# Values times probabilities in column tiles, with row sums on VectorE, one activation table set and shorter 3x3 blocks, in a four-layer convolution kernel

## The chip, the cores and the metric

One core of one Trainium2 chip. The metric is the device time of one execution in microseconds, lower is better. The kernel was timed three times; each time is that of the only core. A profiled execution gives a trace of every instruction on the five engines: TensorE (PE, with its weight loads PEld apart), VectorE (DVE), ScalarE (ACT), GpSimd (POOL) and SyncE (SP, which here only issues DMAs).

## The reference

The input x has shape (4, 384, 64, 64), float32. Four layers follow each other, each as x = x + layer(group_norm(x)) with 32 groups. What the change touches lies in the first three:

```python
# layer 0: attention over 4096 positions on the first 96 channels
q, k, v = qkv[:, :16], qkv[:, 16:32], qkv[:, 32:]          # 16, 16, 96 channels
attn = softmax(einsum('bcn,bcm->bnm', q, k) * scale, axis=-1)
out = einsum('bcn,bmn->bcm', v, attn)
xm = relu(concatenate([out, x_skip], axis=1))               # x_skip: other 288 channels
y = _bn(einsum('oc,bchw->bohw', w_proj, xm))

# layer 1: 1x1, filter in 8x8 Fourier patches, 3x3 depthwise, gated gelu, 1x1
t = einsum(x, w_in); t = irfft2(rfft2(patches(t)) * fft_filter)
t = depthwise3x3(t, w_dw)
g = gelu(t[:, :192]) * t[:, 192:]
return einsum(g, w_out)

# layer 2: depthwise 3x3 and 5x5 side by side, mixed by gates, then an MLP
y3 = _bn(_dw(x, c3_w, 1)); y5 = _bn(_dw(x, c5_w, 2))
tok = _bn(kw[:, 0:1] * y3 + kw[:, 1:2] * y5 + x * c1_w + c1_b)
h2 = _bn(gelu(_bn(tok * gates @ cm_w1)) @ cm_w2)
return gate * (tok * gates + h2) + (1 - gate) * x
```

Layer 3 is a 7x7 depthwise convolution whose kernel depends on the image.

## The kernel before

All arithmetic is in float32. The program is written with tiles and pools; a planner puts the instructions of each engine in an order, by priority (the order of the program, if nothing else is said) and by when it expects their inputs, sets the semaphores, and gives out buffers. On the chip each engine then runs its list in that order. `tc.high_priority()` lifts what is written inside it ahead of older work.

Four stages follow each other.

Attention with layer 1 beside it (`phase_a`, `attention`, `layer1`). For each of four images, 8 blocks of 512 query positions by 8 groups of 512 key positions make 64 steps. A step has:

- scores (L755): four matmuls of 32 contraction rows, each in its own quarter of PE's rows, 128 keys by 512 queries each, into a PSUM tile of four banks that exists once (`p4`, tag "s"). They are written inside `tc.high_priority()`;
- Exp on ACT (L763): two instructions of 128x1024 into `probs` (two buffers). No maximum is subtracted, except where a bound on the weights fails;
- products (L792): four matmuls that accumulate in the PSUM tile `av` (tag "a", two buffers). The stationary operand `vt` is 128 keys by 128 columns: 96 channels of values, and 32 columns of ones, so that rows 96 to 127 of `av` are the sums of the probabilities.

The scores of step n+1 are written ahead of the products of step n. After the eighth key group `finish` takes a reciprocal of the 32 rows of sums (L775) and multiplies it into the 96 rows of values by three instructions of 32 rows (L778); `layer0_end` follows with the projection (L825), the residual (L832) and statistics.

`side_by_side` puts other work between the steps, piece by piece, by a budget in microseconds per step: the statistics of the next image (`x_norm`), its q, k, v (`qkv`), and layer 1 of the image before. Layer 1 works on tiles of 128 positions: `tile_norm` (on DVE, L903, while attention runs; on ACT, L901, for the last image, which has no attention beside it), `tile_hidden` (L911), `tile_filter` (L926, L928), `tile_back` (L936, L939), then `band_taps` with 27 multiply-adds on DVE per band of 8 rows (L988), two gelus (L992, L995), and `band_out` (L1005, L1006, L1009). The PSUM tag "m" that all this shares has two buffers.

The last image's layer 1 alone.

The convolutions of layer 2 (`phase_b`): 12 units of 32 channels, each in 16 rounds of two channels. For a channel, three matmuls (L1196) take a 128x128 piece of the image strips as the stationary operand and banded tap matrices of 256 columns (128 for 5x5, 128 for 3x3) as the moving one. The tap matrices are made on DVE and POOL by turns (`matrices53`, L1177) from compact taps that `_pair` lays out; results leave PSUM by one ACT copy (L1205) and feed statistics (L1208), go to memory, come back in another layout (`unit_tok`, L1261 to L1282) and are mixed.

The MLP of layer 2 (`phase_ef`, L1420, L1472) and layer 3 (`phase_g`).

Every reciprocal root is Ln followed by Exp on ACT (`rsqrt`, L354, L355). The activation tables that ACT needs are loaded by instructions put in at compile time ahead of a function that the loaded set lacks.

Of the kernel before, what the change touches and what calls it, by code (L numbers as in the profile page):

```python
# [40 lines left out]
UNITS = C // 32  # L41

# [154 lines left out]
def _pair(u, v):  # L197

    return np.stack([u, v], axis=4)
# [69 lines left out]
class _Builder:  # L269
# [60 lines left out]

    def open_psum(self, ctx, m_bufs=4):

        self.psum = ctx.enter_context(self.tc.tile_pool(name="psum", bufs=2, space=bass.MemoryType.PSUM))
        self.m_bufs = m_bufs
# [49 lines left out]
    def bn_of_four(self, name, z, g, b, func, out):  # L384
# [8 lines left out]
        nc.scalar.activation(out, z, func, bias=c, scale=a)  # L393
# [31 lines left out]
    def qkv_weights(self, pool):  # L425
# [23 lines left out]
        self.wv = pool.tile([PD + 1, P], F32, tag="wv", name="wv")  # L449
# [3 lines left out]
        nc.gpsimd.memset(self.wv[PD : PD + 1, PD:], 1.0)  # L453
# [3 lines left out]
        nc.vector.tensor_copy(self.wv[:, 0:PD], wt[:, 32:P])  # L457
# [27 lines left out]
    def phase_a(self, strips):  # L485
# [3 lines left out]
        with ExitStack() as ctx:  # L489
            self.open_psum(ctx, 2)  # L490
            cp = ctx.enter_context(tc.tile_pool(name="a_const", bufs=1))
# [20 lines left out]
            self.score_shifts(cp)  # L512
            self.w_proj = self.weight(cp, "w_proj_t")
# [43 lines left out]
    def others(self, b, nxt):  # L557
# [3 lines left out]
        if b + 1 < B:  # L561
            yield from self.x_norm(b + 1)
# [7 lines left out]
    def side_by_side(self, b, steps, others):  # L570

        per_step = ((176 if b else 0) + (42 if b + 1 < B else 0)) / 64
# [74 lines left out]
    def qkv_tiles(self):  # L647
# [4 lines left out]
        vt = self.big.tile([P, 32, P], F32, tag="vt", name="vt", bufs=2)  # L652
        return q, k4, vt

    def qkv(self, b, q, k4, vt):
# [8 lines left out]
        for i in range(8):  # L664
# [18 lines left out]
            mv = m.rearrange("p (c d) -> p c d", d=P)  # L683
# [59 lines left out]
    def attention(self, b, q, k4, vt):  # L743
# [5 lines left out]
        def scores(i, c):  # L749
            p = self.probs.tile([P, 2048], F32, tag="p", name="probs")  # L750
            s = self.p4("sc_s")

            with tc.high_priority():
                for g in range(4):
                    nc.tensor.matmul(  # L755
                        s[:, g],
                        lhsT=k4[32 * g : 32 * g + 32, c],
                        rhs=q[i][32 * g : 32 * g + 32],
                        start=True,
                        stop=True,  # L760
                    )
# [9 lines left out]
        def finish(av):  # L771

            xm = self.work.tile([P, NJ, 512], F32, tag="xm", name="xm", bufs=1)
            rd = self.wk("av_rd", "rd", 1)
            nc.vector.reciprocal(rd[PD:P], av[PD:P])  # L775
            for g in range(3):
                at = slice(32 * g, 32 * g + 32)
                nc.vector.scalar_tensor_tensor(xm[at, 0], av[at], 0.0, rd[PD:P], ALU.max, ALU.mult)  # L778
# [6 lines left out]
        for n_step, (i, c) in enumerate(steps):  # L785
# [3 lines left out]
            if c == 0:  # L789
                av = self.pa("av")  # L790
            for v in range(4):
                nc.tensor.matmul(  # L792
                    av,
                    lhsT=vt[:, 4 * c + v, :],
# [1121 lines left out]
```

## Time and profile before

| | us |
|---|---|
| median of three runs | 4928.02 |
| lowest, highest | 4917.86, 4933.94 |
| profiled execution | 4921.93 |
| its span, first to last instruction | 4920.2 |

| stretch of the profile | from, to (us) | what runs |
|---|---|---|
| prologue | 0 to 128 | constants, first image's statistics and q, k, v |
| attention, four images | 128 to 2225 | steps, with qkv and layer 1 between them |
| last image's layer 1 | 2225 to 2490 | bands, and the first strips |
| convolutions | 2490 to 3095 | 12 units |
| MLP and layer 3 | 3095 to 4920 | |

A group of the profile is a set of instructions of one line, engine, operation and shape, with busy time, mean length of one, and the idle time of the engine just before them with what ended it. Matmuls are pipelined, so the length of one is more than the distance to the next; and a float32 matmul shows as two records. The mean granted TensorE clock was 0.961.

### The profile page before, as it was taken

The numbers are of one execution on the slowest core, as the hardware profiler recorded it, in microseconds if no ns is written. First come the engines' busy times: TensorE is split into PE (matmuls) and PEld (weight loads), VectorE is DVE, ScalarE is ACT, GpSimd is POOL, SyncE is SP. The second block draws the span as 40 slices with busy tenths as digits, with TensorE's granted clock in tenths as the row PEclk, the third lists the DMA queues.
The fourth block names the chain that finished last, engine by engine and source line by source line (L and its number), as shares of the span: only waits on it lengthen the run. The fifth ranks groups of instructions, "written<-read, shape, count | busy, mean of one in ns | idle before, by whom it ended". The sixth has DMA issues, their size and how long they took to land.

```text
span 4920.2 us, 47066 instructions
## 1 busy us (share of the span) xinstructions
PE 4484.3 (91%) x17289; PEld 2510.4 (51%) x17289; DVE 2787.8 (57%) x4506; ACT 2155.9 (44%) x2905; POOL 777.6 (16%) x593
## 2 busy tenths in 40 slices
PE   5999999999999999999978999699999997678988
PEld 2333444334443344435467888344444443577888
DVE  5322566645656345565867778555521113667898
ACT  5444444555445544445245666311123334753321
POOL 1000000000000000000035555000000001225554
PEclk9999999999999999999989999799999998788999
DMA  5210211111122111113259999776664444896776
GB/s 176 69 46 28 92 58 60 61 60 47 56 70 67 47 33 65 65 62 112 83 169 282 288 295 299 250 270 254 250 240 153 154 152 143 309 343 195 234 252 229
DMA packets 345844, 752.21 MB, mean 153 GB/s; under 512 B 22683, under 2 KB 172294, under 8 KB 336646
## 3 DMA queue, kind: packets, MB, share of 16 engines
q1 hardware_dynamic: 279864, 475.07, 31.4%
q0 software_dynamic: 32640, 151.28, 7.9%
q10 hardware_dynamic: 33102, 122.77, 6.4%
q8 instruction: 140, 2.29, 0.2%
q14 instruction: 98, 0.80, 0.1%
HBM read 446.76 MB, written 302.25 MB: 152 GB/s over the span
## 4 chain that ended last, share of the span: by engine, by line
PE 67%; DVE 13%; ACT 8%; DMA 7%; issue 4%; POOL 1%; SPq 0%; ACTq 0%; DVEq 0%; POOLq 0%
PE av L792 14%; PE h_s L1420 10%; PE h_m L1472 9%; PE conv_m L1196 9%; PE sc_s L755 5%; PE proj_m L825 4%; PE t_m L911 3%; DVE acc L988 3%; PE out_m L1006 2%; PE conv_m L1786 2%; PE out_m L1005 2%; PE back_m L936 2%; DMA wmix<-in_mix_t 1%; ACT probs L763 1%; DMA g_h<-h 1%
## 5 line engine op out<-in xcount | busy, mean ns | idle before, releaser
L792 PE MATMUL av<-probs,vt 128*128 128x512 f32 x2048 | 964.6, 606 | 0.1
L763 ACT ACTIVATE probs<-sc_s 128x1024 f32<-128x1024 f32 x512 | 501.1, 1021 | 721.3 <-PE av L792 717.9
L792 PEld LDWEIGHTS av<-probs,vt 128*128 128x128 f32 x2048 | 369.7, 192 | 467.9 <-issue 460.5
L1196 PE MATMUL conv_m<-toep,z 128*128 128x256 f32 x2304 | 520.1, 385 | 10.3 <-DVE toep L1177 6.4
L988 DVE SCALAR_TENSOR_TENSOR acc<-band,vecs,acc 128x512 f32<-128x512 f32 x708 | 496.6, 746 | 45.7 <-POOL band L949 40.0
L1472 PE MATMUL h_m<-f_h,cm_w_t 128*128 128x512 f32 x1152 | 496.6, 594 | 8.8 <-ACT f_h L1462 8.7
L1196 PEld LDWEIGHTS conv_m<-toep,z 128*128 128x128 f32 x2304 | 439.0, 193 | 71.7 <-DVE z L1129 4.9
L1786 PE MATMUL conv_m<-toep,z 128*128 128x128 f32 x3072 | 391.4, 285 | 40.5 <-POOL toep L1773 21.6
L1786 PEld LDWEIGHTS conv_m<-toep,z 128*128 128x128 f32 x3072 | 377.0, 201 | 42.8 <-POOL toep L1773 22.0
L1177 POOL TENSOR_TENSOR toep<-w,band 128x1536 f32<-128x1536 f32 x94 | 323.8, 3445 | 281.7 <-PE conv_m L1196 240.8
L1420 PE MATMUL h_s<-e_tok,cm_w_t 128*128 128x512 f32 x768 | 362.6, 594 | 5.5 <-DMA e_tok<-tok 5.5
L1472 PEld LDWEIGHTS h_m<-f_h,cm_w_t 128*128 128x128 f32 x1152 | 219.3, 191 | 286.1 <-issue 273.5
L755 PE MATMUL sc_s<-q,k 32*128 32x512 f32 x2048 | 296.5, 648 | 25.7 <-ACT probs L763 25.2
L1480 DVE BATCH_NORM_STATS2 h_st<-f_h 128x6 f32<-128x512 f32 x96 | 66.4, 694 | 429.2 <-ACT f_h L1479 429.2
L911 PE MATMUL t_m<-w_in_t,xb 128*128 128x384 f32 x768 | 276.4, 494 | 4.7 <-DVE coef L928 3.5
L825 PE MATMUL proj_m<-xm,w_proj_t 128*128 128x512 f32 x576 | 269.4, 606 | 9.4 <-DVE xm L778 6.5
L1427 ACT COPY e_h<-h_s 128x1024 f32<-128x1024 f32 x96 | 97.2, 1012 | 400.8 <-PE h_s L1420 400.8
L832 DVE SCALAR_TENSOR_TENSOR x_res<-proj_m,bn_c,x_res 128x512 f32<-128x512 f32 x96 | 71.7, 747 | 308.7 <-PE proj_m L825 308.7
L1420 PEld LDWEIGHTS h_s<-e_tok,cm_w_t 128*128 128x128 f32 x768 | 146.5, 191 | 189.7 <-issue 183.6
L1429 DVE BATCH_NORM_STATS2 h_st<-e_h 128x6 f32<-128x512 f32 x192 | 123.5, 685 | 199.5 <-ACT e_h L1427 199.5
L911 PEld LDWEIGHTS t_m<-w_in_t,xb 128*128 128x128 f32 x768 | 142.3, 191 | 141.0 <-issue 58.0
L1420 PE MATMUL h_s<-z,cm_w_t 128*128 128x512 f32 x384 | 196.1, 592 | 0.0
(392 smaller groups left out, 6119.3 us busy)
## 6 DMA issues: line engine op xcount, KB each, us to landing
d<-d_o ACTq DMA_DIRECT2D x96, 512.0 KB
c_d<-d SPq DMA_DIRECT2D x96, 512.0 KB
hid<-e_h ACTq DMA_DIRECT2D x16, 3072.0 KB
f_h<-hid SPq DMA_DIRECT2D x16, 3072.0 KB
x_in<-in_x SPq DMA_DIRECT2D x96, 256.0 KB
x_res<-in_x SPq DMA_DIRECT2D x32, 768.0 KB
xa<-x_res POOLq DMA_DIRECT2D x32, 768.0 KB, 3.9
xa_in<-xa SPq DMA_DIRECT2D x32, 768.0 KB
```

The lines of the kernel that those rows point to most:

```text
L755: nc.tensor.matmul(s[:, g], lhsT=k4[32 * g : 32 * g + 32, c], rhs=q[i][32 * g : 32 * g + 32], start=True, stop=True,)
L763: nc.scalar.activation(p[:, h * 1024 : (h + 1) * 1024], s[:, 2 * h : 2 * h + 2].rearrange("p a b -> p (a b)"), AF.Exp, scale=0.25,)
L792: nc.tensor.matmul(av, lhsT=vt[:, 4 * c + v, :], rhs=p[:, v * 512 : (v + 1) * 512], start=c == 0 and v == 0, stop=c == 7 and v == 3,)
L825: nc.tensor.matmul(m, lhsT=self.w_proj[:, j, o * P : (o + 1) * P], rhs=xm[:, j], start=j == 0, stop=j == NJ - 1,)
L911: nc.tensor.matmul(m[:, 0:C], lhsT=xb[:, j], rhs=self.w_in[:, j, :], start=j == 0, stop=j == NJ - 1,)
L988: nc.vector.scalar_tensor_tensor(out, src(j, k), w, done, ALU.mult, ALU.add)
L1177: eng.tensor_tensor(t, self.w53[:, at : at + 192].rearrange("p (m n) -> p m n", n=8).unsqueeze(2).to_broadcast([P, 24, 8, 8]), band.rearra ...
L1196: nc.tensor.matmul(m[:, c * 256 : (c + 1) * 256], lhsT=self.z_[:, at : at + P], rhs=t[:, 12 * c + 4 * i : 12 * c + 4 * i + 4].rearrange("p ...
L1420: nc.tensor.matmul(s[:, v, :], lhsT=w1[:, j, o * P : (o + 1) * P], rhs=t[j][:, v * 512 : (v + 1) * 512], start=j == 0, stop=j == NJ - 1,)
L1429: nc.vector.bn_stats(st[:, o, 8 * b + 2 * i + v, :], h[:, o, v * 512 : (v + 1) * 512])
L1472: nc.tensor.matmul(m, lhsT=w2[:, o, j * P : (j + 1) * P], rhs=h[:, o, v * 512 : (v + 1) * 512], start=o == 0, stop=o == 5,)
L1786: nc.tensor.matmul(m[:, ch * P : (ch + 1) * P], lhsT=self.z_[:, at : at + P], rhs=t[:, 8 * c + 2 * i : 8 * c + 2 * i + 2].rearrange("p m a ...
```

## The change

Products and sums. `vt` and `wv` lose the ones columns and are 96 wide. Each step's products are twelve matmuls of 32 columns in place of four of 128: each one of four key groups times one of three quarters of the values. A plan says which go together, one in each quarter of PE's columns, in three rounds, and into which of two PSUM tiles each accumulates.

```diff
+PLAN = (
+    ((0, 0, 3), (0, 1, 2), (0, 2, 1), (0, 0, 0)),
+    ((1, 1, 0), (0, 1, 3), (0, 2, 2), (0, 0, 1)),
+    ((1, 1, 1), (1, 2, 0), (0, 2, 3), (0, 0, 2)),
+)
...
+        def products(av, c, p):
+            quarter = lambda g: slice(32 * g, 32 * g + 32)
+            for n, jobs in enumerate(PLAN):
+                for g, (k, s, v) in enumerate(jobs):
...
+                    nc.tensor.matmul(
+                        av[k][quarter(g)],
+                        lhsT=vt[:, 4 * c + v, quarter(s)],
+                        rhs=p[:, v * 512 : (v + 1) * 512],
...
+        def add_up(c, p):
+            lo, hi = p[:, 0:1024], p[:, 1024:2048]
...
+                nc.vector.tensor_add(self.acc, self.acc, lo)
+                nc.vector.tensor_add(self.acc, self.acc, hi)
+            if c == 7:
...
+                nc.vector.tensor_add(self.prob_sum, self.acc[:, 0:512], self.acc[:, 512:1024])
```

At the end of a block the two PSUM tiles are copied out by two ACT and two DVE copies at high priority; the sums over partitions are made by four matmuls with a block of ones, laid out as 128x128, inverted by one reciprocal, and spread again over 96 partitions and 512 columns by four matmuls with a broadcast identity column. Two DVE instructions then add the halves and multiply.

```diff
+        def evacuate(av):
+            a, t = self.wk("av_a", "rd", 1), self.wk("av_t", "av_t", 1)
+            with tc.high_priority():
+                nc.scalar.copy(t[0:32], av[0][96:128])
+                nc.vector.tensor_copy(a[0:PD], av[0][0:PD])
+                nc.scalar.copy(t[32:64], av[1][0:32])
+                nc.vector.tensor_copy(t[64:96], av[1][32:64])
+            return a, t
+        def invert(total):
+            m = self.pm("sum_m")
+            for g in range(4):
+                nc.tensor.matmul(
+                    m[32 * g : 32 * g + 32, 0:P],
+                    lhsT=self.ones,
+                    rhs=total[:, g * P : (g + 1) * P],
...
+            rd = self.sm([P, P], "av_rd")
+            nc.vector.reciprocal(rd, m[:, 0:P])
-            rd = self.wk("av_rd", "rd", 1)
-            nc.vector.reciprocal(rd[PD:P], av[PD:P])
-            for g in range(3):
-                at = slice(32 * g, 32 * g + 32)
-                nc.vector.scalar_tensor_tensor(xm[at, 0], av[at], 0.0, rd[PD:P], ALU.max, ALU.mult)
+            m = self.pm("rd_m")
+            for g in range(4):
+                nc.tensor.matmul(
+                    m[0:PD, g * P : (g + 1) * P],
+                    lhsT=self.ident[:, 32 * g : 32 * g + 1].to_broadcast([P, PD]),
+                    rhs=rd,
...
+            nc.vector.tensor_add(t[0:PD], t[0:PD], a[0:PD])
+            nc.vector.scalar_tensor_tensor(xm[0:PD, 0], t[0:PD], 0.0, m[0:PD], ALU.max, ALU.mult)
...
-                av = self.pa("av")
+                av = self.pa("av_0"), self.pa("av_1")
```

The scores are no longer written at high priority. `tile_norm` runs on ACT for all images. The statistics of images 1 and 2 are made beside image 0, those of image 3 beside image 1, and the budget follows:

```diff
-        if b + 1 < B:
-            yield from self.x_norm(b + 1)
+        for later in ((1, 2), (3,), (), ())[b]:
+            yield from self.x_norm(later)
...
-        per_step = ((176 if b else 0) + (42 if b + 1 < B else 0)) / 64
+        per_step = ((172 if b else 0) + (38 if b + 1 < B else 0) + (8, 4, 0, 0)[b]) / 64
```

Tables. The set that holds both Exp and Ln is loaded on purpose at the start, and again behind the last use of any other set (gelu, sigmoid, square root). A band's two gelus stand together, behind the third tap group:

```diff
+    def ln_exp(self, behind=None):
+        load = lambda: self.nc.scalar.preload_act_table_set("natural_log_exp_and_others")
...
-            if j == 1:
-                nc.scalar.activation(acc[0], acc[0], AF.Gelu)
-                nc.vector.tensor_mul(acc[1], acc[1], acc[0])
             if j == 2:
-                nc.scalar.activation(acc[0][64:P], acc[2][0:64], AF.Gelu)
-                nc.vector.tensor_mul(acc[2][64:P], acc[2][64:P], acc[0][64:P])
+                g = self.wk("gelu", "gelu", 1)
+                with self.tc.high_priority():
+                    first = nc.scalar.activation(g[64:P], acc[2][0:64], AF.Gelu)
+                    with self.tc.issue_after(first.ins):
+                        last = nc.scalar.activation(acc[0], acc[0], AF.Gelu)
+                    self.ln_exp(last)
+                nc.vector.tensor_mul(acc[1], acc[1], acc[0])
+                nc.vector.tensor_mul(acc[2][64:P], acc[2][64:P], g[64:P])
```

Convolutions. Of the twelve tap blocks of a channel two were zero for the 3x3; `_pair` now lays out ten, a channel's middle matmul has 256 columns and the two outer ones 192, and the results leave PSUM by two copies.

```diff
-            for i in range(3):
+            for i, k0, k1, to in ((1, 3, 7, 0), (0, 0, 3, 0), (2, 7, 10, 64)):
...
-                    m[:, c * 256 : (c + 1) * 256],
+                    m[:, c * 256 + to : c * 256 + to + 64 * (k1 - k0)],
...
-        nc.scalar.copy(self.d_o[:, :, at : at + 2], mv)
+        nc.scalar.copy(self.d_o[:, 0, at : at + 2], mv[:, :, 64:192])
+        ends = mv.rearrange("p c (k n) -> p c k n", n=64)[:, :, 0:4:3]
+        nc.scalar.copy(self.d_o[:, 1, at : at + 2].rearrange("p c (f n) -> p c f n", f=2), ends)
```

## The prediction

> **What bounds the kernel now.** I read the busy shares first, then the same by stage, then the groups inside the two stages that the change touches, then the order of time for what one step costs.
>
> ```profile
> PE 4484.3 (91%) x17289; PEld 2510.4 (51%) x17289; DVE 2787.8 (57%) x4506; ACT 2155.9 (44%) x2905; POOL 777.6 (16%) x593
> DMA  5210211111122111113259999776664444896776
> ```
> ```profile
> 128.00:560.00 432.00, 413.74 (x1334) 164.79 (x1334) 139.09 (x236) 199.26 (x225) 8.82 (x14) 0.98 0.18 57
> 585.00:1110.00 525.00, 504.25 (x1649) 216.54 (x1648) 312.52 (x511) 259.87 (x317) 20.01 (x39) 0.99 0.17 58
> 1110.00:1690.00 580.00, 559.55 (x1842) 242.65 (x1841) 330.60 (x574) 288.37 (x354) 23.28 (x44) 0.99 0.17 57
> 1690.00:2225.00 535.00, 518.31 (x1690) 223.29 (x1688) 296.33 (x481) 232.02 (x283) 16.13 (x34) 0.98 0.17 56
> 2225.00:2490.00 265.00, 236.72 (x784) 121.21 (x784) 196.44 (x320) 113.47 (x215) 11.85 (x26) 0.94 0.32 106
> 2490.00:3095.00 605.00, 568.21 (x2718) 492.01 (x2718) 455.58 (x878) 360.00 (x557) 323.81 (x94) 0.97 0.91 271
> ```
> The columns are stretch, length, busy PE, weight loads, DVE, ACT, POOL, granted clock, DMA share, GB/s. The first four rows are the four batches of attention: PE 96 to 97%, DVE 32% in the first and 55 to 60% in the others, ACT near 50%. The fifth is the last image's band work alone, the sixth the 5x5 and 3x3 convolutions: PE 94%, DVE 75%, DMA 91%. So a microsecond of PE work is a microsecond of span, until DVE or DMA has no room.
>
> ```profile
> L792 PE MATMUL av<-probs,vt 128*128 128x512 f32 x2020 | 949.1, 605 | 0.0
> L763 ACT ACTIVATE probs<-sc_s 128x1024 f32<-128x1024 f32 x502 | 491.2, 1021 | 721.2 <-PE av L792 717.9 <-PE sc_s L755 2.5
> L755 PE MATMUL sc_s<-q,k 32*128 32x512 f32 x2000 | 287.4, 644 | 24.5 <-ACT probs L763 23.9
> L775 DVE RECIPROCAL av_rd<-av 32x512 f32<-32x512 f32 x32 | 107.6, 3363 | 93.0 <-PE av L792 92.7
> L778 DVE SCALAR_TENSOR_TENSOR xm<-av,av_rd 32x512 f32<-32x512 f32 x96 | 65.6, 684 | 1.9
> L763 ACT ACT_TABLE_LOAD x44 | 56.5, 1283 | 0.8
> ```
> These are groups of the attention stretch. An f32 matmul is two records. Exp waits for PE (717.9 us), PE waits for Exp 23.9 us only: PE is the bound, ACT is not.
>
> ```profile
> 1200.49 2.74 PE L825 MATMUL proj_m<-xm,w_proj_t 128*128 128x512 f32 x6
> ...
> 1203.15 1.14 PE L755 MATMUL sc_s<-q,k 32*128 32x512 f32 x8
> ...
> 1204.22 2.20 PE L911 MATMUL t_m<-w_in_t,xb 128*128 128x384 f32 x6
> ...
> 1207.77 3.60 PE L792 MATMUL av<-probs,vt 128*128 128x512 f32 x8
> ...
> 1211.20 2.74 PE L825 MATMUL proj_m<-xm,w_proj_t 128*128 128x512 f32 x6
> ```
> Start, length, count. One step's eight av records take 1211.20 - 1207.77 = 3.43 us, 0.428 each. The score group is four row tiles: eight records in one block. The proj records before it are through at 1200.49 + 6 x 0.428 = 3.06 past 1200, the next matmul starts at 4.22: the block costs 1.16 us against 2 x 0.428 = 0.86 for perfect overlap. So four tiles do run at once, and entering plus leaving the tiled form costs 0.30.
>
> ```profile
> 2730.42 20.89 PE L1196 MATMUL conv_m<-toep,z 128*128 128x256 f32 x96
> ```
> ```profile
> 4890.10 4.47 PE conv_m L1786 x40
> ```
> A 256-column record streams at 20.89/96 = 0.218 us; a 128-column one, with its own weights each time, at 0.112. Weight loads therefore keep up with records of 0.112, and a 192-column record should take 0.163.
>
> **What the Trainium skill says.** "TensorE: Matmul & The Clock Gate", Measured speedup vs the span model: four row tiles give 3.07x, three column tiles 2.38x, column within some ns of row. The trace has 3.43/1.16 = 2.96 for four row tiles; it has no column tiles that run together. "TensorEngine Tiling (Array Packing)", Key Properties: a change of tiling mode drains the array; the 0.30 above fits. "ScalarE: Activation LUTs", Table sets: exp and ln have one set in common, and a switch costs 2.66 us with its drain; the trace has 1283 ns and the next ACTIVATE right behind. "VectorE: DVE Perf Modes", Mode 2x_2P: an fp32 tensor_tensor cannot use two ports for one tensor, so 128x1024 takes twice a 128x512, which is 681 ns at L993.
>
> **The change, part by part**, against the profiled execution (4921.9; span 4920.2).
>
> *Products.* 256 steps (4 batches x 8 x 8) lose 3.43 us and gain three rounds of four column tiles. Best case 3 x 0.857 = 2.57; with the mode change of the score block 2.87; some groups stand next to scores and share the change. I take 2.83: 256 x 0.60 = -153. Bounds: 2.57 gives -220; three rounds that each drain like the score block, 3 x 1.16 = 3.48, give +13.
> *Sums.* The ones columns go, DVE adds instead: two 128x1024 adds a step, about 1.21 us each (1.14 apart, as the chain of L988 has 0.746 at 0.678 spacing), 256 x 2.42 less the shorter first step: about +600 us of DVE, 150 a batch. Gone from DVE: half-empty reciprocals 107.6 (now 128 wide, a quarter of the length, some 27), two of three L778 (-41), the band norm of L903 (82.5, to ACT); added: two PSUM copies and one add per block, 32 x 2.1 = 65. Second batch: 312 + 106 = some 420 of about 500 us, 84%; third and fourth 76 to 80%. DVE stays under PE, but its queue is in order and carries tap chains of 6 us (1208.91: nine in 6.10), so coef (L928), x_res (L832) and the release of the probs buffers come later and PE waits now and then: +25, between 0 and +90.
> *Inversion and spread on PE.* Per block eight 128-column records for rd_m at 0.112 to 0.157, and eight in column tiles for the sums, 0.22 + 0.30: about 1.5 us x 32 = +48 (35 to 60). The narrower v_m stays at its weight loads: 0.
> *Evacuation.* av now takes both "a" banks, so a block's first product waits for two ACT copies (0.58) and two DVE copies (0.68) of the block before. Behind that product stand all later PE instructions. A score block and a piece of other work, 1.1 + 3 us, cover it; if DVE is in a chain they don't: +8 (0 to 50).
> *Tables.* 144 loads in the attention stretch become some 48 (two for each of 24 bands): -123 us of ACT, given back by the band norm (288 x 0.43 = +124) and evacuation (+37). ACT stays at 50%. PE's 23.9 us of waits for Exp fall to about 14: -10. Before 128 us, 22 loads go, some on the chain of the first layer norms: -8. The twelve loads after 3095 stand in serial statistics: -6. In the stretch alone each band now loads twice, 16 x 1.28 = 20 us of ACT at 43%, and both gelus come at the end: +4 (0 to 15).
> *Scores unprioritized, budget, earlier x_norm.* Scores no longer cut an av group in two (they do at 1241.07), which saves a second mode change that column tiles would pay. No work is added; the 23.9 could rise instead: within the bounds above.
> *3x3 blocks.* A channel has 256 + 192 + 192 columns in place of 3 x 256. Two of three tap groups shrink by 0.218 - 0.163, two records each: 384 x 4 x 0.055 = -84 of PE. Beside it toep falls by a sixth, the split d_o copy costs ACT +30 (two of 0.37 for one of 0.584) against 28 loads of 1.28 that mostly go. Left after PE: DVE (455 - 28)/521 = 82%, and DMA: 164 MB in 521 us is 315 GB/s against 271 mean, 292 in the middle and 390 at best in 4 us stretches. Taken -60 (-15 to -85).
> Sum: -153 + 25 + 48 + 8 - 10 - 8 - 6 + 4 - 60 = -152. The profiled execution becomes 4770; the median of the runs shown lies 6 above it, so 4776.
>
> **Rivals.** (1) *DVE takes the bound in attention.* For it: 84% in an in-order queue, and every probs buffer (two) now waits for DVE too. Against: its sum is under PE's in each batch. Waits of 110 instead of 25: 4861. (2) *The convolutions become DMA-bound.* For it: DMA share 0.91, 0.99 in the middle. Against: DVE, ACT and POOL wait there for DMA some 33 us in all, PE hardly, and the share reads 1.2 in places, so it is no ceiling. The gain shrinks to 15: 4821. (3) *Slower: the column tiles overlap less than row tiles do.* Place: the product groups; each tile streams its own 128-partition operand, which row tiles don't. It decides from 3.42 us a step (2.83 + 152/256), that is 1.14 a round, hardly below the measured score block, so three rounds that drain each time suffice: 4776 + 256 x 0.65 = 4942. Two at a time, 5.44, give 5444; no overlap, 24 x 0.428 = 10.3, gives 6688. Against it only the skill's 2.38x.
>
> **Chances.** Forecast 0.69, rival 1 0.09, rival 2 0.07, rival 3 0.15. The forecast's bounds: all gains 4640, most costs 4900; that holds rivals 1 and 2, and leaves out rival 3 and a little. A measurement tells about 0.3% from no change. Faster 0.82 (the first three, less a sliver), within 0.3% 0.03, slower 0.15.
>
> **What would show it.** A product group should be 24 records of 32 columns in about 2.6 to 2.9 us; DVE adds near 1.2 us; DVE at 80 to 85% in batches two to four; ACT loads near 50 in attention; conv records of 192 columns at 0.163 and the stage near 545 us. Wrong: rounds of over 1.1 us; PE waits for DVE over 60 us; DMA waits in the convolutions; PE idle at each block's start before the first product.

## The result, and the profile after

The changed kernel takes 4958.01 us (median; 4943.58 to 4968.24) against 4925.86 for the kernel before on the same chips: ratio 1.0064, interval 1.0047 to 1.0080. It is slower by 0.6% where a gain of 3% was forecast. The profiled execution takes 4950.78 us (span 4948.9) against 4921.93 for the kernel before.

First the busy shares of the changed kernel (engine, busy time, share, instructions; then the DMA share over the span), then the same by stage with the columns of the stage rows shown before the result. The first four rows are the batches of attention, the fifth the last image's bands alone, the sixth the convolutions.

```profile
PE 4430.6 (90%) x21897; PEld 2370.8 (48%) x21897; DVE 3215.2 (65%) x4762; ACT 2127.7 (43%) x3310; POOL 731.0 (15%) x593
DMA  4410111111111111112349999876654444896776
```
```profile
128.00:560.00 432.00, 395.58 (x2577) 128.48 (x2574) 290.35 (x397) 191.57 (x247) 17.40 (x23) 0.95 0.22 69
560.00:1110.00 550.00, 518.09 (x2744) 195.05 (x2743) 411.99 (x563) 261.08 (x382) 20.39 (x40) 0.97 0.17 57
1110.00:1700.00 590.00, 555.82 (x2963) 208.88 (x2964) 426.77 (x589) 286.15 (x427) 22.17 (x43) 0.95 0.17 56
1700.00:2240.00 540.00, 505.32 (x2852) 190.46 (x2851) 384.73 (x499) 261.10 (x386) 15.19 (x30) 0.96 0.15 52
2240.00:2556.00 316.00, 270.47 (x854) 133.55 (x853) 225.53 (x361) 136.98 (x234) 16.51 (x30) 0.89 0.31 100
2556.00:3125.00 569.00, 502.13 (x2683) 464.20 (x2682) 426.92 (x867) 331.74 (x713) 272.39 (x94) 0.93 0.92 278
```

PE is still the bound: 92 to 94% busy in attention, DVE at 67 to 75%. But attention is not shorter, and the granted clock fell from 0.99 to 0.96 there and from 0.97 to 0.93 in the convolutions. Next, the groups of the changed kernel's attention stretch (busy time, mean ns of one, idle time before and what ended it).

```profile
L801 PE MATMUL av<-probs,vt 128*32 128x512 f32 x6076 | 745.1, 618 | 10.8 <-DVE av_t L829 7.7 <-DVE av_a L827 3.1
L786 ACT ACTIVATE probs<-sc_s 128x1024 f32<-128x1024 f32 x504 | 487.6, 1018 | 427.9 <-PE sc_s L778 402.5 <-DVE acc_p L817 15.5 <-DVE xa_st L629 7.7
L778 PE MATMUL sc_s<-q,k 32*128 32x512 f32 x2016 | 363.5, 664 | 8.9 <-ACT probs L786 8.8
L817 DVE TENSOR_TENSOR acc_p<-acc_p,probs 128x1024 f32<-128x1024 f32 x221 | 270.0, 1222 | 16.0
L816 DVE TENSOR_TENSOR acc_p<-acc_p,probs 128x1024 f32<-128x1024 f32 x221 | 269.9, 1221 | 166.1 <-ACT probs L786 165.6
```

The products fell from 949.1 us to 745.1: the column tiles do what was forecast. The scores, which issue exactly what they did before, rose from 287.4 us to 363.5. The order of time in one step of the changed kernel (start, length, engine, count, idle time before) shows how.

```profile
1218.79 0.91 PE L1003 MATMUL coef_m<-t_t,to_coef 128*128 128x384 f32 x2 [1.59 <-DVE x_res L912]
1219.63 1.13 PE L778 MATMUL sc_s<-q,k 32*128 32x512 f32 x6
1221.23 0.94 PE L1013 MATMUL back_m<-to_pos,coef 128*128 128x128 f32 x6 [0.47 <-ACT t_t L996]
1222.10 1.12 PE L778 MATMUL sc_s<-q,k 32*128 32x512 f32 x2
1223.15 2.78 PE L801 MATMUL av<-probs,vt 128*32 128x512 f32 x24
1225.86 2.84 PE L905 MATMUL proj_m<-xm,w_proj_t 128*128 128x512 f32 x6
```

One step's group of 24 product records takes 1225.86 - 1223.15 = 2.71 us. The score block of eight records is cut into six and two, with six records of a band's `back_m` between them: the piece of two takes 1223.15 - 1222.10 = 1.05 us, as long as a whole block. With the priority gone, the ordering of the instructions fills other TensorE work in between the four row tiles of a block.

The table takes each kernel's trace from the first score to the last product. A run is a stretch of records of one tile with no other between them (`av` counts as one tile); it is timed from its first record to the start of the next run, or to its own end where TensorE then idles. The last column is half of the busy time that falls into stretches with the TensorE clock at one half (the clock record knows only full and half); it lies inside the other columns. The fourth column has the number of score runs and their time. All times are us, of one profiled execution each. Some expectations quote counts that differ a little from this one, such as 777 for the products of e1 and 913 for those of e11.

| kernel | attention | products | score runs, time | PE idle | lost to half clock |
|---|---|---|---|---|---|
| before | 2136 | 923 | 256, 279 | 81 | 28 |
| after | 2177 | 737 | 318, 362 | 139 | 97 |
| after, scores in priority (e1) | 2116 | 783 | 256, 279 | 113 | 37 |
| before, scores without (e2) | 2269 | 937 | 311, 357 | 91 | 92 |
| after, sums left out (e3) | 2154 | 734 | 319, 363 | 118 | 97 |
| before, tables alone (e5) | 2111 | 919 | 256, 277 | 61 | 27 |
| before, products alone (e8) | 2182 | 805 | 256, 278 | 146 | 54 |
| e1 with a fixed order (e9) | 2087 | 770 | 256, 276 | 118 | 41 |
| before, tables, short 3x3, norm on ACT (e11) | 2108 | 917 | 256, 277 | 62 | 24 |
| e1, sums left out (e12) | 2086 | 785 | 256, 278 | 89 | 22 |

### The profile page after: what moved, and what is told of

It is laid out like the page before. It is cut to its first block, busy times and chain, and to the rows that moved or that the text cites. A ratio compares the mean times of both kernels' runs of the same rounds, so it can differ in the third digit from the quotient of the medians.

```text
span 4948.9 us, 57215 instructions
## 1 busy us (share of the span) xinstructions
PE 4430.6 (90%) x21897; PEld 2370.8 (48%) x21897; DVE 3215.2 (65%) x4762; ACT 2127.7 (43%) x3310; POOL 731.0 (15%) x593
## 5 line engine op out<-in xcount | busy, mean ns | idle before, releaser
L801 PE MATMUL av<-probs,vt 128*32 128x512 f32 x6144 | 758.3, 619 | 10.8 <-DVE av_t L829 7.7
L1276 PE MATMUL conv_m<-toep,z 128*128 128x192 f32 (+1 forms) x2304 | 447.1, 356 | 17.9 <-DVE toep L1257 17.7
L801 PEld LDWEIGHTS av<-probs,vt 128*32 128x32 f32 x6144 | 178.9, 112 | 549.2 <-issue 510.3
L1276 PEld LDWEIGHTS conv_m<-toep,z 128*128 128x128 f32 x2304 | 410.7, 197 | 40.9 <-issue 10.1
L1873 PEld LDWEIGHTS conv_m<-toep,z 128*128 128x128 f32 x3072 | 381.6, 203 | 38.2 <-POOL toep L1860 18.7
L778 PE MATMUL sc_s<-q,k 32*128 32x512 f32 x2048 | 381.6, 666 | 8.9 <-ACT probs L786 8.8
L816 DVE TENSOR_TENSOR acc_p<-acc_p,probs 128x1024 f32<-128x1024 f32 x224 | 273.6, 1221 | 167.4 <-ACT probs L786 166.8
L1257 POOL TENSOR_TENSOR toep<-w,band 128x1280 f32<-128x1280 f32 x94 | 272.4, 2902 | 310.1 <-PE conv_m L1276 196.5
L817 DVE TENSOR_TENSOR acc_p<-acc_p,probs 128x1024 f32<-128x1024 f32 x224 | 273.6, 1221 | 16.0
```

Of the source, the lines that this page charges most:

```text
L778: nc.tensor.matmul(s[:, g], lhsT=k4[32 * g : 32 * g + 32, c], rhs=q[i][32 * g : 32 * g + 32], start=True, stop=True,)
L801: nc.tensor.matmul(av[k][quarter(g)], lhsT=vt[:, 4 * c + v, quarter(s)], rhs=p[:, v * 512 : (v + 1) * 512], start=c == 0 and not before, s ...
L816: nc.vector.tensor_add(self.acc, self.acc, lo)
L817: nc.vector.tensor_add(self.acc, self.acc, hi)
L1276: nc.tensor.matmul(m[:, c * 256 + to : c * 256 + to + 64 * (k1 - k0)], lhsT=self.z_[:, at : at + P], rhs=t[:, 10 * c + k0 : 10 * c + k1].r ...
L1873: nc.tensor.matmul(m[:, ch * P : (ch + 1) * P], lhsT=self.z_[:, at : at + P], rhs=t[:, 8 * c + 2 * i : 8 * c + 2 * i + 2].rearrange("p m a ...
```

## Experiments on attention

Times are medians; each ratio is to the kernel before on the same chip.

**e1: priority back.** The changed kernel with one line more.

```diff
+            with tc.high_priority():
                 for g in range(4):
```

> The changed kernel with the priority of the score matmuls put back, nothing else. Theory A (the scores, left to the planner without priority, are cut into pieces by other TensorE work, and each piece pays entering and leaving the tiled form again): runs of score records go back from some 307 to about 250, their slot time from 345 us to about 270, and the half-clock stretches shrink with them; the kernel takes 4830 to 4890 us, 1 to 2.5% under the changed kernel. Theory B (DVE's in-order queue with 570 us of added sums makes TensorE wait, and each wait drops its clock): the waits for DVE stay near 100 us and the clock stays low; 4935 to 4965. A second rival to A: with priority the score blocks land inside the groups of products, which now pay the change of form twice as well; then the product groups grow from 2.71 us a step by what the score runs save, and the time stays within 0.3%.

4899.43 us, ratio 0.9945 (0.9929 to 0.9962). Theory A has the mechanism right: no score block is cut, their time is back at 279 us, the half clock costs 37 us, not 97, and TensorE's waits that DVE ended fall from 104 us to 86. The time lies 9 us above its range. The one line is worth 59 us: with it the change gains 28 us. The second rival has a share in it: products rise from 737 to 783, chiefly because score blocks now fall into product groups. The order of time of this kernel:

```profile
1525.16 1.90 PE L802 MATMUL av<-probs,vt 128*32 128x512 f32 x10
1526.99 1.14 PE L779 MATMUL sc_s<-q,k 32*128 32x512 f32 x8
1528.07 1.92 PE L802 MATMUL av<-probs,vt 128*32 128x512 f32 x14
1529.91 2.84 PE L906 MATMUL proj_m<-xm,w_proj_t 128*128 128x512 f32 x6
```

The two pieces take 1.83 and 1.84 us, 3.67 in place of 2.71: a cut costs 0.96 us here. What a piece costs follows the rounds that it begins, not its records (a round is four matmuls, eight records). Mean time of a run at full clock, by its records (us):

| run of | 2 | 4 | 6 | 8 | 10 | 14 | 16 | 24 |
|---|---|---|---|---|---|---|---|---|
| new products (e1) | 0.98 | - | 0.99 | 1.03 | 1.85 | 1.85 | 1.89 | 2.72 |
| old products (before) | 0.98 | 1.84 | 2.65 | 3.49 | | | | |
| scores (changed kernel) | 1.06 | 1.09 | 1.08 | 1.07 | | | | |

Two records one after another are 2 x 0.428 = 0.86. So a run of tiled matmuls costs about 0.86 for each round that it begins, plus 0.1 to 0.2 once. A cut inside a round makes one round into two, 10 + 14 records 3.70 in place of 2.72; a cut between rounds, 8 + 16, adds only 0.20; and in the old products, where nothing overlaps, 4 + 4 adds 0.19. The price of a cut is mostly lost overlap.

**e2: priority taken from the kernel before.** The reverse edit.

> The kernel before with the priority of the score matmuls taken away, nothing else: this part of the change alone. Theory A: the score blocks are split here as well, 40 to 80 more runs of about 1.05 us each, so 4965 to 5010 us, 0.8 to 1.7% slower than before. The prediction's own reading (no work is added, and product groups are cut less often): within 0.4% of before, 4910 to 4945. If splitting only comes with the changed kernel's other work (more small TensorE instructions that become ready between two halves of a score block), also within 0.4%.

5057.46 us, 1.0272 (1.0255 to 1.0289): 130 us slower, more than any theory gave. 55 more score runs cost 78 us of their own time; with them comes a half clock in 25 stretches in place of 13, and the small band groups around them lengthen. The products rise from 923 to 937, though whole groups rise from 132 to 245. So the edit costs more on the old products than on the new, which it spares 46 us. The prediction's reading ("no work is added") is excluded.

**e3: sums left out.**

```diff
-            else:
-                nc.vector.tensor_add(self.acc, self.acc, lo)
-                nc.vector.tensor_add(self.acc, self.acc, hi)
```

> The changed kernel without the sums of seven of the eight key groups: DVE adds only the first group of each block, so the probabilities are divided by the sum over 512 of 4096 keys. This takes about 224 x 2.42 = 540 us from DVE in the attention stretch and a reader of each probs buffer. Theory B: idle TensorE in attention falls from 137 to about 70 us and the half-clock loss there from 74 to some 25 us: 4840 to 4870 us. Theory A: the score runs stay at about 307 and 345 us, the time falls by no more than the waits for DVE, 20 to 50 us: 4905 to 4935.

4923.69 us, 0.9987 (0.9976 to 0.9999), that is 34 us under the changed kernel. The kernel leaves out seven of the eight key groups' sums. Idle fell by 21 us and the half-clock loss stayed at 97. Theory B is rejected as the main cause: taking 540 us from DVE gains 34.

**e8: products alone.** Products, sums, inversion, evacuation and the 96-wide `vt` in the kernel before; scores in priority, tables, band norm and budget as before.

> The kernel before with the new products, sums, inversion and evacuation alone; scores keep their priority, tables, band norm, budget and convolutions are those of before. The prediction's terms for this part: -153 + 25 + 48 + 8 = -72, so 4854, ratio 0.985. If column tiles pay for being cut by priority scores as the run above suggests (about +40 on 723 us of products) and the waits for DVE drop the clock: 4880 to 4910. If DVE, here with the band norm still on it (82 us) and 570 us of sums, takes the bound in the last three batches: above 4930.

4982.67 us, 1.0125 (1.0102 to 1.0147): 58 us slower where the prediction's terms give 72 less. By the count of the table, which has not all tiles: products -118, `rd_m` and `sum_m` +50, idle +65, and the rest in longer band groups (`t_m` 192 to 205, `back_m` 75 to 84). So TensorE's busy time falls by only 19 us (2055 to 2036), and the waits take more than that back. The longest of them, in the attention stretch of this kernel, and three in the kernel before (from 128 us to 2225; who waits, for whom: total us, times, longest):

```profile
PE sc_s L763 <- ACT probs L771: 26.3, 30, 3.4
PE back_m L1001 <- ACT t_t L984: 24.4, 14, 2.6
PE av L786 <- DVE av_t L814: 13.1, 4, 9.8
PE v_m L693 <- ACT ln_rs L361: 8.8, 8, 2.7
```
```profile
PE sc_s L755 <- ACT probs L763: 23.9, 27, 2.9
PE v_m L685 <- ACT ln_rs L354: 9.5, 6, 2.7
PE back_m L936 <- ACT t_t L919: 5.5, 5, 1.5
```

Three of the four longest are for ACT, but two of the three stood there before. Summed over attention by the engine that ended them, the waits for ACT rise from 48 us to 63 (`back_m` alone by 19), and those for DVE from 31 to 81, spread over many small ones. So most of the rise is for DVE. It is 76 to 77% busy in batches two to four, so its rate isn't the bound: the third expectation has the time right and the mechanism wrong.

**e5: tables alone.**

> The kernel before with the table part of the change alone: Ln and Exp loaded as one set, both gelus of a band moved to its last step, the set loaded again behind them; the band norm stays on DVE. As predicted (waits for Exp -10, prologue -8, statistics after the convolutions -6, last image's bands alone +4), 20 us less: 4907, ratio 0.996. If the late gelus and the load behind each of them are what lengthens the last image's bands in the changed kernel by some 20 us, this one has that too: its stretch alone 290 to 300 us against 274 and the time 4925 to 4935. If that stretch is longer for another reason (what is left over of the bands when attention ends), it stays at 270 to 278.

4892.41 us, 0.9932 (0.9908 to 0.9955): 32 us less, 25 of it in attention. The bands alone take 291 us against 274: most of what that stretch loses in the changed kernel comes with the late gelus and the load behind each band.

**e9: a fixed order.** e1, where each score block is queued behind the whole product group of the step before, and each product group behind the score block of the next step.

```diff
-            with tc.high_priority():
+            with tc.high_priority(), self.behind(self.last_product):
...
+                    with self.behind(last_score):
```

> The changed kernel with scores in priority, and the order of the two tiled blocks fixed: each score block is queued behind the whole product group of the step before, each product group behind the whole score block of the next step, so neither is ever cut by the other. If what the products lose in that kernel is the cuts (777 us of product slots against 737 uncut, and the half-clock stretches beside them): product runs all of 24, 735 us, the time 4850 to 4875. If a fixed order only moves the loss into waits (a score block that waits for its product group, Exp later, idle TensorE up from 114 us): 4890 to 4930.

4867.84 us, 0.9886 (0.9869 to 0.9902): 32 us under e1. 199 of 256 groups stay whole, against 123 in e1; score blocks hardly cut any, but `v_m`, `back_m` and other small groups still do. The products gain 13 us (783 to 770) of the 40 expected; `sum_m` gains 8 (19 to 11), `t_m` 5, `proj_m` 4, the rest is spread thinly. Idle is hardly up, so the order itself costs no waits.

**e10 and e11: what is there without the products.** e10 is the kernel before with tables and short 3x3, and in the last image's bands the gelus as they were; e11 also moves the band norm to ACT.

> The kernel before with the tables and the short 3x3 blocks, and in the last image's bands alone the gelus where they were before and no load behind each band; products, sums, scores, band norm as before. If the parts add up (tables -32, convolutions -12 in the runs above, and the 17 us of the stretch alone given back): 4865, ratio 0.988. If the stretch alone is not lengthened by the gelus: 4880.

> The same with the band norm on ACT. In that kernel DVE has no sums to do, so taking 82 us from it should be worth little: within 12 us of the run before it. If ACT's share (the norm stands in ACT's queue between two Exps, and t_m waits for it) costs TensorE waits: 15 to 40 us more. If DVE's queue was what held the bands' instructions back even before the change: 15 to 30 us less.

4865.25 us, 0.9872 (0.9856 to 0.9889), and 4864.82 us, 0.9872 (0.9855 to 0.9888). The parts add up, the stretch alone is back at 279 us in both, and the norm's move is worth nothing with the old products. These two are as fast as e9 without any column tile (e9 still has the late gelus, 299 us in the stretch alone).

**e12: e1 with the sums left out.**

> The changed kernel with scores in priority and without the sums of seven of the eight key groups (DVE adds only the first group of each block; the division is by the sum over 512 of 4096 keys). Against the run with scores in priority and all sums (4899): if DVE's queue causes the idle TensorE that is still there (114 us against 61 with the tables alone), idle falls to 60 to 80 us and the time to 4840 to 4865. If the sums are covered here too: within 20 us of 4899, that is 4880 or above.

4878.90 us, 0.9897 (0.9879 to 0.9916), 20 us under e1: at the border of the two expectations. Idle went from 113 to 89, half-clock loss from 37 to 22. The sums are worth about 20 us in the repaired kernel, no more.

**e14: the old products in the fixed order.** e11 with the edit of e9.

> The kernel before with tables, short 3x3 blocks, band norm on ACT and the last image's gelus as before (4865 us in the run above), and now the same fixed order of the two tiled blocks: old products of 128 columns, sums on TensorE. If the cuts cost the old products too (913 us of product slots against 256 x 3.44 = 880 uncut): about 35 us less, 4830, and the new products are then worth at most 20 us over the old ones at the same order. If in the old products a score block inside a group costs nothing more (two changes of form in any place): within 10 us of 4865, and the new products in the same order are worth 15 to 20 us.

4897.18 us, 0.9942 (0.9923 to 0.9961), 32 us slower than e11: neither expectation. Their groups of four matmuls stay whole in 205 cases against 144, and the products still take 933 us, not less than the 917 of e11, as the small price of a cut in the old products lets one expect; `coef_m` waits 29.7 us for DVE's `x_res`. So the old products run better with free priority and the new ones with the fixed order; each at its better, attention takes 2108 us (e11) and 2087 (e9). The new products are worth about 21 us there, not 72. e9 also has the changed budget and the earlier `x_norm`, which were not tried apart.

## Experiments on the convolutions

The stage, from the first `conv_m` record to the last, went from 591 us to 567. The `conv_m` records, each counted to the start of the next and brought to full clock, fell from 501.7 us to 421.4. Of these 80 us, 33 went into idle TensorE (32 us to 65) and 24 into the half clock (11 to 35). Two of TensorE's waits in the convolutions, before and after:

```profile
PE strip_m L1124 <- ACT unit_x L1117: 1.8, 1, 1.8
PE conv_m L1196 <- DVE toep L1177: 6.4, 5, 3.0
```
```profile
PE strip_m L1204 <- ACT unit_x L1197: 26.4, 10, 4.0
PE conv_m L1276 <- DVE toep L1257: 17.7, 7, 4.9
```

Then those of SP's queue, before and after:

```profile
SPq L1282 <- DVE c_d L1274: 126.1, 31, 10.4
SPq L1282 <- DVE st L1208: 52.6, 8, 10.6
SPq L1261 <- DMA d<-d_o: 86.7, 22, 9.7
```
```profile
SPq L1364 <- DVE st L1290: 159.5, 34, 11.0
SPq L1343 <- DMA d<-d_o: 103.9, 39, 8.2
SPq L1190 <- DMA d<-d_o: 24.9, 8, 7.8
```

L1364 (L1282 before) stores a finished token tile and waits on SP for DVE, about as long before the change as after it; the loads of the strips (L1190), the results (L1343) and the taps (L1243) stand behind it.

**e4: short 3x3 alone.**

> The kernel before with the short 3x3 convolution alone (ten tap blocks in place of twelve, 192-column records, the split copy of the result), nothing else. As predicted, 60 us less: 4866 (0.988). As the changed kernel's trace has it, 24 us less in that stretch: 4902 (0.995). If the stretch loses its gain to the order of SP's queue (loads of the taps stand behind stores that wait for DVE), the TensorE records sum to some 57 us less here too, and POOL waits for the taps; if it loses it to the changed kernel's lower clock and not to the order, this one comes near 4870 with a stage near 550 us.

4914.99 us, 0.9977 (0.9966 to 0.9988): 12 us less. The records do sum to 80 us less at full clock (501.7 to 421.8); idle rose from 32 to 70 us and the half-clock loss from 11 to 44. So the gain is lost inside this stage, without the rest of the change.

**e6: taps fetched two groups ahead** (e1 as base; `taps53(n + 8)`, three buffers).

> The changed kernel with scores in priority (4899 us in the run above), and the taps of the convolutions fetched two groups ahead (a third buffer) in place of one. If the convolutions' lost gain comes from the taps being late behind stores on SP's queue: POOL's 62 us of waits for the taps fall under 15, idle TensorE in the stretch from 49 to some 30 and its half-clock loss from 43 to about 20, the stretch from 576 to about 535 and the time to about 4860. If POOL is off the path: POOL's waits go, the time stays within 10 us of 4899.

4895.09 us, 0.9938 (0.9922 to 0.9955). POOL's waits for the taps fell to 18 us, from 49.5 in e1, and the time by 4: POOL is off the path. The waits of `strip_m` for the strips rose instead, from 25.2 us to 38.6.

**e7: one copy of the result** (e1 as base).

```diff
+        nc.scalar.copy(self.d_o[:, at : at + 2], m.rearrange("p (c k n) -> p c k n", c=2, k=4))
```

> The changed kernel with scores in priority, and the result of the short 3x3 blocks copied from PSUM by one ACT instruction in place of two, in the order in which TensorE wrote it; the statistics read it strided and the second half leaves in two DMAs of 64 columns. If ACT's extra copy (12 x 16 x 0.37 = 71 us, less what the single copy costs more) makes ACT reach the norm of the next strips late, which is what TensorE waits for most in this stretch (strip_m for unit_x, 26 us): those waits fall under 8 and the stretch from 576 to about 545. If not, no change, or slower by the smaller DMA pieces: 570 to 590.

4922.76 us, 0.9998 (0.9989 to 1.0007): the stage is longer, 592 us against 576. The ACT copy was not what made the strips late; whether the smaller DMA pieces or the strided statistics cost the 16 us was not tried.

**e13: the store off SP's queue** (base e9, gelus of the last image as in e10).

```diff
-            nc.sync.dma_start(self.tok[u, :, :, sl].rearrange("b c n -> (b c) n"), d5)
+            nc.scalar.dma_start(self.tok[u, :, :, sl].rearrange("b c n -> (b c) n"), d5)
```

> The changed kernel with the fixed order of score blocks and product groups (4868 us in the run above), the last image's gelus where they were before with no load behind each band, and the store of the finished token tile issued from ACT's queue in place of SP's, so that no load of the convolutions stands behind a store that waits for DVE. The stretch alone gives back some 18 us (299 to about 281) in any case: 4850. If the convolutions' lost gain is the order of SP's queue: TensorE's waits for the strips (27 to 39 us) and POOL's for the taps fall under 10 each, the stretch from 571 to about 540 and the time to about 4820. If the strips are late because ACT and DVE themselves are late: the stretch stays at 565 to 575. If ACT's queue now holds its own copies back behind a store: 580 or more.

4838.11 us, 0.9816 (0.9800 to 0.9833). The stage falls from 571 us to 545, where the prediction had put it, and the last image's bands from 299 us to 287. TensorE's and SP's waits in the stage: nothing on SP stands behind the store of DVE's tokens now, and the wait for the strips is down from 24.9 us in e9 to 14.7. But `cn_rep`, for DVE's statistics, now waits 24.4 us in place of 4.0.

```profile
PE cn_rep L1324 <- DVE st L1305: 24.4, 10, 4.3
PE strip_m L1219 <- ACT unit_x L1212: 14.7, 9, 3.2
```
```profile
SPq L1258 <- POOL toep L1272: 88.1, 27, 4.1
SPq L1358 <- DMA d<-d_o: 82.2, 25, 8.5
SPq L1358 <- DMA tok<-c_d: 46.5, 12, 8.9
```

**e15 and e16: the control.** The same store moved in the kernel before, with the long 3x3 blocks and with the short ones.

> The kernel before with the store of the token tile issued from ACT's queue, nothing else. If that order only binds once TensorE is faster (TensorE idles 26 us in the stretch there): within 8 us of before, the stretch 585 to 592. If the order costs the long 3x3 blocks just as much, so that the gain seen with the short ones has nothing to do with them: 20 to 30 us less, the stretch near 565.

> The kernel before with the short 3x3 blocks and that store on ACT's queue. The prediction's 60 us for the short blocks alone should now show: the stretch 591 to about 545 and the time 4870 to 4880, against 4915 with the store on SP. If the short blocks are worth nothing more than the order: the same as the run before it.

4939.87 us, 1.0032 (1.0019 to 1.0044), and 4894.24 us, 0.9939 (0.9919 to 0.9960). Both miss their ranges. For the long blocks the move costs 19 us, not under 8, and the stage takes 601.5 us; for the short ones it gains 19 (0.9977 to 0.9939), not 35 to 45, and the stage falls from 581 us to 563, not 545. So the short blocks are worth 46 us with the store on ACT and 12 with it on SP, but 19 of the 46 only make good what the move costs the long ones. The order is a gain only once TensorE is faster. With the short blocks it takes the waits for the strips from 28.0 us to 11.8 and brings those of `cn_rep` from 4.0 to 23.7. Their stage rows, e16 and then e13 (columns as above):

```profile
2494.00:3057.00 563.00, 501.58 (x2683) 465.43 (x2682) 423.46 (x863) 355.29 (x734) 272.38 (x94) 0.93 0.93 280
```
```profile
2463.00:3008.00 545.00, 492.78 (x2683) 459.17 (x2684) 422.14 (x864) 326.14 (x710) 272.56 (x94) 0.93 0.96 290
```

The same transfers ran at 271 GB/s in e4 and at 290 in e13: in e4 they had at least that much room.

## Why the prediction was wrong, step by step

- **Scores unprioritized: the step that failed.** The prediction took "No work is added; the 23.9 could rise instead". The waits for Exp did fall (8.8 us), and product groups are cut less (737 us against 783 with priority), as it said. But the score blocks themselves are cut, at 1.05 us for each extra piece, and the clock is at half more often. e1 prices the line at 59 us on the new kernel, e2 at 130 on the old one. It was costed at 0 in a forecast of -152. The prediction did see cuts, of product groups, but priced one at a change of mode, 0.30; the runs show that a cut inside a round costs a round, about 1 us. This step makes the sign: with the priority kept (e1), the change gains 28 us. That is still far from 152, so two more terms below, marked mis-sized, failed too.
- **Products.** -153 forecast; the runs give 737 - 923 = -186 uncut and -140 with priority. 2.71 us a step lies below the 2.83 taken. Rival 3 (overlap less than row tiles) is excluded.
- **Waits beside the products: mis-sized.** +25 was taken for DVE, up to +90 allowed. Waits that DVE ended rise from 31.3 us to 80.6 in e8 (+49) and to 103.8 in the changed kernel (+72), past the sign of being wrong that the prediction gave itself (over 60 us). The sums are only part of it: leaving them out takes 34 us from the changed kernel (e3) and 20 from e1 (e12), and waits for DVE still stand at 84 us in e3 and 54 in e12. Which of DVE's other new work holds TensorE up was not tried. Waits for ACT rise by 15 us in e8, for which the prediction had nothing beyond `av`. Rival 1 (DVE as the bound, 4861) is excluded: its busy time came as forecast (412 us in the second batch, for some 420), and its share only to 71 to 75% in batches two to four, because the batch took 550 us and not 500. Its adds took 1.22 us, as summed (the doubling quoted beside the citation would give 2 x 0.681 = 1.36).
- **Inversion and spread.** +48 forecast, +50 in e8 and +41 in the changed kernel. Evacuation: +8 forecast, 10.8 us of `av` waits for it.
- **Tables.** -20 in all forecast, -32 in e5. Its one loss was too small: "+4" for the stretch alone is +17 in e5 and +21 in the changed kernel, and e10 gets 12 of the 17 back by leaving the gelus of the last image where they were.
- **3x3: mis-sized.** "Taken -60 (-15 to -85)", measured -12 alone and -24 in the changed kernel's stage. The PE term was right: 80 us at full clock against 84. What it missed is that the strips and the tap matrices come late for a faster TensorE, +33 us idle, and that the clock then falls, +24. What is late next was sought in DMA's rate (rival 2, 4821); a share of it is the order of one queue, 19 us by e16. The rest stays open; in e16 the longest wait is `cn_rep` for DVE's statistics. The time in e4 came near rival 2's "gain of 15" by luck: TensorE and ACT hardly wait for a DMA there.
- **The clock.** The prediction held the granted clock for constant. Inside attention its loss rose from 28 to 97 us, in the convolutions from 11 to 35. In attention it goes with the cut score blocks: e1 brings it back to 37 and e2 raises it from 28 to 92.

By parts: tables -32, short 3x3 -12 and products +58, each alone on the kernel before, and the priority line +59 on the changed kernel make +73; the whole change gave +32. The 41 us between come from parts that help one another: e1, which has all but the line, is 28 us under the kernel before, where the first three terms give +14. A likely one is that the table part takes loads from ACT: waits that ACT ended are 63 us in e8 and 26 in e1, a fall of 38, where the tables alone take 18 from the kernel before (48 to 30). Another would be that the band norm on ACT takes 82 us from a DVE that has the sums; the waits for DVE, 81 us in e8 and 86 in e1, don't show it. Neither pair was tried without the rest, nor were the budget and the earlier `x_norm`.

e13 beats both kernels: 1.8% under the kernel before. It keeps the whole change, puts the scores back in priority, fixes their order against the products, leaves the last image's gelus in place and stores the tokens from ACT's queue. Little of it may be due to the column tiles: e11, without them, has 4864.82 us with the store on SP, and if the move gains there the 19 us that it gains with the short blocks alone, it would come to some 4846 (an estimate from e4 and e16; that kernel was not run).

## What to carry to other kernels

An edit that issues the same instructions can still cost the most: where blocks of tiled matmuls share TensorE with other work, price each cut (here a whole round, about 1 us, when it falls inside one) and ask who decides the order. When a stage's bound engine is made faster, look in the in-order DMA queues for a transfer that waits for compute ahead of loads that need not. Test each part of a bundle alone and with the line that orders it, since the same part can read as 12 us in one order and 46 in another.

## What was not expected of the hardware

- Four column tiles overlap almost wholly: 24 records, three rounds in a row, take 2.71 us. At 0.428 a record one after another they would take 10.3, so the factor is 3.8. A run of one round alone takes 1.03 (e1), against 1.07 for the score block of four row tiles, so the two kinds hardly differ. The Trainium skill, "TensorE: Matmul & The Clock Gate", Measured speedup vs the span model, has 2.38 for three column tiles, 0.79 of the three; here it is 0.95 of the four over three rounds and, at 1.03, 0.83 of the four in one, and the measurement decides.
- A piece of two score records takes 1.05 us, one of eight 1.07: one tile takes as long as four. Only 0.2 of it is beyond the 0.86 of its two records.
- The half clock doesn't need idle time. The same page, What's actually happening, names an idle window of about 3.4 us. In the kernel before, each of 12 such stretches in attention follows at least 1.6 us of idle TensorE in the 7 us ahead; in the changed kernel 10 of 29 follow less than 1.5 us, two of them none, and a stretch lasts 7.7 us on average, not 4.6. From 1052 us to 1060 TensorE is busy for all 8.00 us, and the clock goes to one half at 1058.3 (the ends of matmuls are modelled in the trace, so short idle times may be hidden). That pieces of tiled work count as little activity is only argued.
